# A graph layer with a 17-tap convolution: another start for the first four batches, single conv taps in a ring of nine, and fewer turns of the identity

## The chip, the cores and the metric

The kernel runs on one core of one Trainium2 chip. The metric is the time of one execution on the device in microseconds, the median of several runs. A profiled execution is one more run, taken with the hardware profiler; its trace gives the span from the first to the last instruction. "TensorE" (PE) does matmuls and turns (transposes by a matmul with the identity), "VectorE" (DVE) and "ScalarE" (ACT) elementwise work, "GpSimd" (POOL) small work and DMA issues, "SyncE" (SP) most DMA issues.

## The reference

The layer takes x (32 batches of 512 nodes with 256 channels) and an adjacency matrix of 512x512 for each batch. Everything is fp32. Cut to what is computed:

```python
h  = maximum(layernorm(x), 0)                  # no scale, no shift
xc = transpose(h, (0, 2, 1))                   # channels x nodes
c  = relu(bn1(conv1d(xc, conv1_w, pad=0)))     # 1 tap, 256 -> 256
c  = bn2(conv1d(c, conv2_w, pad=8))            # 17 taps, 256 -> 256
x_conv = transpose(relu(c + xc), (0, 2, 1))
s    = h @ w_se.T + b_se                       # 3 numbers for each node
dist = sq[:, :, None] + sq[:, None, :] - 2 * einsum('bnd,bmd->bnm', s, s)
A    = exp(-dist) * adj                        # sq: sums of s * s
msg  = relu(h @ w_msg.T + b_msg)
x_nmp = einsum('bnm,bmd->bnd', A, msg)
x_in = concatenate([x_conv, x_nmp], axis=-1)
# a GRU cell with input x_in and state h: gates r, z, n
out  = x + (1 - z) * n + z * h
```

## The kernel before

**The parts.** A batch passes through these: `norm` (statistics on VectorE, reciprocal root on GpSimd, the affine on ScalarE, in place), the turn from nodes to channels on the partitions (`norm_t`, L141 on TensorE for the first eight batches, on VectorE for later ones), conv1 (`conv1`, names `ps_g<-hT,w`; its eviction by ScalarE writes `h`), the graph (`graph`: messages `ps_g<-wmsg,hTg`, small factors, four tile-positioned matmuls of 5 rows at L917, `exp` by ScalarE into `at`, four masks multiplied on VectorE, then the gather `ps_g<-at,msg`), and the gates (`gates`, names `ps_acc`).

**The 17-tap convolution** runs over groups of batches. `STARTS` cuts all columns of all batches into seven stages; the first holds four batches (`G = 4`). Within a stage it is a two-level fast convolution: 25 products (`ORDER` x `ORDER`), each with its own combination of inputs (`X2`, made by `operands` on VectorE, names `x`) and its own combination of the weights (`w`). In the first stage the weights are made on the fly by VectorE (`g`, `gg`, from `wraw`), scaled by ScalarE and stored to `WD` in device memory; in later stages they are loaded again. A product has weights 0 and 1, and from the second stage on also their sum, 2, which `third_weight` makes on VectorE once and GpSimd's queue stores. One product, number 6 (`LONE`), needs weight 1 alone. A tile `w` holds all three weights of one product, and three tiles rotate:

```python
    def new_w():
        return cv.tile([P, 3, ND, D], F32, name="w", bufs=3)
```

**The order of the work** is made by a planner that runs when the program is built. Each part is a Python generator, a "stream" (`rows`, `begins`, `graphs`, `conv`, `gates`); the main loop (L1390 and on) picks the stream with the lowest clock among those that are ready by the planner's own estimate of time, `now`, and that stream writes its next instructions into the queues. `fill` adds background work to VectorE's queue while its estimated end is less than 1.5 us ahead: norms, weights (`prepare_some`, at most 3 products ahead), operands (`operand_some`, at most `AHEAD = 3` ahead). Each engine then executes its own queue strictly in that order.

When no stream is ready, `now` goes on by 0.25 us, and until the gates begin TensorE gets turns of the identity into an unused bank (`keep_warm`, L146):

```python
            waits += 1
            if waits > 2 and not HB:
                keep_warm(2)
```

**The start.** Before the loop the planner norms batch 0, then makes the constants of the two batch norms (`bn_affine`, which needs `vecs` loaded and GpSimd's power), then loads batches 1 to 3 (2 and 3 into the space of `y`). The stream `rows` begins with, for each of the first four batches in turn: `begin` (the norm, the two `norm_t`), a wait for ScalarE, then conv1 of that batch. Batch 2 also waits until batch 0's messages are out (`told > 0`). The tile `hT` rotates through two buffers.

**Banks.** TensorE's results for turns, conv1, messages, exps' inputs and gathers share three banks (`gps`), the gates three (`acc`), the convolution two (`cps`, one in the first stage for each product).

Of the kernel before, what the change touches and what calls it, by code (L numbers as in the profile page):

```python
# [8 lines left out]
F32 = mybir.dt.float32  # L9
AF = mybir.ActivationFunctionType  # L10
ALU = mybir.AluOpType
PSUM = bass.MemoryType.PSUM

P = 128
# [35 lines left out]
def kernel(  # L50
# [228 lines left out]
        dve.tensor_scalar(t[:, :n], var, EPS, None, op0=ALU.add)  # L279
        nc.gpsimd.tensor_tensor(dst, t[:, :n], mhalf[:, :n], op=ALU.pow)  # L280

    def bn_affine(name):

        g, bb, m, v = (vec[:, _COL[f"{name}_{k}"] : _COL[f"{name}_{k}"] + ND] for k in "gbmv")
        sc = const.tile([P, ND], F32, name=f"{name}_scale")
        sh = const.tile([P, ND], F32, name=f"{name}_shift")
        rs = front.tile([P, ND], F32, name="bn_rs")
        rsqrt(rs, v)
        dve.tensor_tensor(sc, g, rs, op=ALU.mult)
        t = front.tile([P, ND], F32, name="bn_t")  # L290
        dve.tensor_tensor(t, m, sc, op=ALU.mult)
        dve.tensor_tensor(sh, bb, t, op=ALU.subtract)
        return sc, sh


    h1 = const.tile([P, Q * RV], F32)
# [52 lines left out]
    def norm(b):  # L349

        xs = XS[b]
        st = front.tile([P, NT, 6], F32, name="st")
        mv = front.tile([P, NT, 2], F32, name="mv")
        rstd = front.tile([P, NT], F32, name="rstd")
        shift = front.tile([P, NT], F32, name="shift")
        step = NT // 2 if b == 0 else NT
        for c in range(NT):
            dve.bn_stats(st[:, c, :], xs[:, c, :])
            dve.bn_aggr(mv[:, c, :], st[:, c, :])
            if (c + 1) % step == 0:  # L360
                rsqrt(rstd[:, c + 1 - step : c + 1], mv[:, c + 1 - step : c + 1, 1])
            if c % 2:
                yield dve.free + 2.0 if c == NT - 1 else 0.0
        for c0 in range(0, NT, step):
            k = slice(c0, c0 + step)
            dve.scalar_tensor_tensor(
                shift[:, k], mv[:, k, 0], -1.0, rstd[:, k], op0=ALU.mult, op1=ALU.mult
            )
            yield dve.free + 0.2
            for c in range(c0, c0 + step):  # L370
                act.activation(
                    xs[:, c, :], xs[:, c, :], AF.Identity if b < TURNED else AF.Relu,
                    bias=shift[:, c : c + 1], scale=rstd[:, c : c + 1],
                )
                if c % 2:
                    yield act.free + LAG
# [108 lines left out]
    def operands(g):  # L485

        rv = sizes(g)[3]
        h = h1[:, : Q * rv].rearrange("p (q e) -> p q e", q=Q)
        for x1 in fives(h, 6, rv, lambda: phases("x1", 6, rv, 2), again=True):
            yield None  # L490
            if x1 is not None:
                yield from fives(x1, 2, rv, lambda: phases("x2", 2, rv, 6))

    def ends(x2, rv):

# [25 lines left out]

    WS, W_AT = [], []

    def new_w():
        return cv.tile([P, 3, ND, D], F32, name="w", bufs=3)

    def weights_first():


        outer = [  # L530
            taps_of(
                lambda k, i=i: wraw[:, i, :, :, k, :],
                lambda i=i: prep.tile([P, 2, 3, D], F32, name=f"g{i}", bufs=1),
                True,
            )
            for i in range(ND)
        ]
        for j1 in ORDER:
            g = []
            for o in outer:  # L540
                g.append(next(o))
                yield 0.0
            inner = [
                taps_of(
                    lambda k, i=i: g[i][:, :, k, :],
                    lambda i=i: prep.tile([P, 2, D], F32, name=f"gg{i}", bufs=2),
                    False,
                )
                for i in range(ND)
            ]  # L550
            for j2 in ORDER:
                gg = []
                for i in range(ND):
                    gg.append(next(inner[i]))
                    yield 0.0
                yield dve.free + 0.1
                w = new_w()
                for i in range(ND):
                    act.activation(
                        w[:, :2, i, :], gg[i], AF.Copy, scale=GSCALE[j1] * GSCALE[j2]  # L560
                    )
                nc.scalar.dma_start(WD[len(WS)][:, :2], w[:, :2])
                WS.append(w)
                W_AT.append(act.free + LAG)
                yield 0.0

    def weights_again(m):

        w = new_w()
        k = slice(1, 2) if m % 25 == LONE else slice(0, 2 if m < 50 else 3)  # L570
        nc.sync.dma_start(w[:, k], WD[m % 25][:, k])
        WS.append(w)
        W_AT.append(now + 7.0)

    thirds = set()

    def third_weight(m):
        if m in thirds or m % 25 == LONE:
            return
        thirds.add(m)  # L580
        w = WS[m]
        dve.tensor_tensor(w[:, 2], w[:, 0], w[:, 1], op=ALU.add)
        later(dve.free + 0.4, lambda: nc.gpsimd.dma_start(WD[m % 25][:, 2], w[:, 2]))
        W_AT[m] = dve.free + LAG

    SUMS = []
# [136 lines left out]
            evacuated[b] = PARTS[-1]  # L723
        return True

    AHEAD = 3
    HB_AT, gating = {}, 0
    XC, XC_AT, RES, evacuated = {}, {}, {}, {}
    X2, X_AT, XD = [], [], {}
# [27 lines left out]

    def prepare_some():
        nonlocal prepare_at
        if len(WS) >= 25 or len(WS) >= at_product + 3 or now < prepare_at:  # L760
            return False
        prepare_at = next(prepare)
        return True

    def convolution():
# [3 lines left out]
        def product(ps, *terms, clear=(True, True)):  # L769


            for o in range(ND):
                pairs = [
                    (w[:, k, i, o * P : (o + 1) * P], t[:, at + i * (nu + 1) : at + i * (nu + 1) + nu])
                    for k, t, at in terms
                    for i in range(ND)
                ]
                for n, (lhsT, rhs) in enumerate(pairs):
                    matmul(
                        ps[:, o * nu : (o + 1) * nu], lhsT, rhs,  # L780
                        start=(n == 0 and clear[o]), stop=(n == len(pairs) - 1),
                        skip_group_check=True,
                    )
# [10 lines left out]
        for g in range(NG):  # L794
# [9 lines left out]
            for n in range(25):  # L804
                at_product = m = 25 * g + n
                if n == 6:
                    yield lambda: not EVAC
                while 25 <= len(WS) < min(m + 2, 25 * NG):
                    weights_again(len(WS))
                if m == 24:  # L810
                    yield lambda: len(WS) >= 25
                if late is None and len(WS) >= 25:
# [23 lines left out]
                else:  # L836
                    in_product = True
                    ps = [bank_[:, :nh] for bank_ in pair]
                    if n == LONE:
                        for k in range(2):  # L840
                            product(ps[k], (1, x2[:, 1 - k, :], k), clear=(True, False))
                    else:
                        product(ps[0], (2, x2[:, 1, :], 0), clear=(True, False))
                        act.activation(ps[1], ps[0], AF.Copy)
                        yield act.free + LAG
                        if 25 <= len(WS) == m + 2 < 25 * NG:
                            weights_again(m + 2)
                        for k in range(2):
                            product(ps[k], (k, XD[m][:, k, :], 0), clear=(False, False))
                        del XD[m]  # L850
# [2 lines left out]
                if g > 0:  # L853
                    later(now + 0.3, hand)
                at_product = m + 1
                if 25 <= len(WS) == m + 2 < 25 * NG:
                    weights_again(m + 2)
                yield now
                if g > 0:
                    yield lambda: done is None  # L860
# [109 lines left out]
    def begin(b):  # L970
# [4 lines left out]
        if b >= TURNED:  # L975
# [19 lines left out]
            if b + 2 < B:  # L995
                later(now + 2.0, lambda: load(b + 2))
            return
        if b == 2:
            yield lambda: told > 0
        yield lambda: b not in NORMS  # L1000
        yield NORM_AT[b]
        turning = True
# [292 lines left out]
    def all_graphs():  # L1295
        for b in range(B):
            yield from graph(b)

    def all_begins():
        for b in range(G, B):  # L1300
            yield lambda: b in XS and not rows_wait
            yield from begin(b)
# [1 line left out]
    rows_wait = turning = False  # L1304

    def all_rows():
        nonlocal rows_wait
        for b in range(G):
            yield from begin(b)
            yield act.free + LAG  # L1310
            yield from rows(0, b)
        for g in range(1, NG):
            for b in batches(g):
                yield lambda: (
# [13 lines left out]
    def all_gates():  # L1328
# [5 lines left out]


    streams = {
        "rows": (all_rows(), 1e9, -2.0),
        "begins": (all_begins(), 1.05 * PER, -0.15),
        "graphs": (all_graphs(), 11.5 * PER, -0.5),
# [11 lines left out]
    while 0 in NORMS:  # L1351
        NORM_AT[0] = next(NORMS[0], -1.0)
        if NORM_AT[0] < 0.0:
            del NORMS[0]
    bn1_sc, bn1_sh = bn_affine("bn1")
    bn2_sc, bn2_sh = bn_affine("bn2")
    brz = const.tile([P, 2 * ND], F32)
    dve.tensor_tensor(
        brz, vec[:, _COL["b_ih"] : _COL["b_ih"] + 2 * ND], vec[:, _COL["b_hh"] : _COL["b_hh"] + 2 * ND],
# [5 lines left out]
    dve.tensor_scalar(  # L1365
        bn, vec[:, _COL["b_hh"] + 2 * ND : _COL["b_hh"] + 3 * ND], 0.5, None, op0=ALU.mult
    )
    NORM_AT[0] = act.free + LAG
    load(1)
    spare = cv.tile([P, 9 * NZ], F32, name="y")  # L1370
    for b in (2, 3):
        at = (b - 2) * NT * D
        load(b, spare[:, at : at + NT * D].rearrange("p (c d) -> p c d", d=D))
    nc.sync.dma_start(wmsg[:, :, :D], w_msg)
    nc.sync.dma_start(wmsg[:, :, D:], w_se)
    nc.sync.dma_start(bmsg[:, :D], b_msg.to_broadcast([P, D]))
# [6 lines left out]
    while streams:  # L1383
        names = [k for k in streams if hold[k] is None or hold[k]()]
        able = [k for k in names if ready[k] <= now]
        if not able:
            now += 0.25
            assert now < 1e4
            waits += 1
            if waits > 2 and not HB:  # L1390
                keep_warm(2)
            fill()
            continue
        name = min(able, key=lambda k: clock[k])
# [64 lines left out]
```

## Time and profile before

| | |
|---|---|
| three runs | 2067.52, 2068.64, 2070.0 us; median 2068.64 |
| profiled execution | 2070.59 us |
| its span | 2068.8 us |
| mean granted TensorE clock | 0.994 |
| VectorE, ScalarE busy | 64%, 40% of the span |
| DMA | 378.31 MB, mean 183 GB/s |
| identity turns (L146) | 142, 21.9 us by the profile's modelled ends |
| first 17-tap product starts | 57.5 us |
| waits of TensorE with a named releaser | 15.5 us in all, the two longest 1.8 us each |

How to read it: a group of the timeline starts at its first column and is as long as its second; neighbouring matmuls overlap in the record, since they are pipelined and their ends modelled. The pace of a kind of matmul is therefore read from one group's start to the next group's start. One fp32 matmul appears as two records, a turn as one.

### The profile page before, as it was taken

To read this page: it belongs to the slowest core of one execution; us is meant where nothing else is said; L and a number is where in the kernel's file an instruction comes from. 1 tells how busy PE (TensorE), PEld (TensorE's weight loads), DVE (VectorE), ACT (ScalarE), POOL (GpSimd) and SP (SyncE) were. 2 spreads that over 40 slices of the span, in tenths; PEclk is the share of its full clock that TensorE was granted. 3 is DMA by queue.
4 is the path that set the end of the run, shared out by engine and by line. 5 is a ranking of instruction groups with operands and counts; after the bars stand their busy time and mean duration, and the time that the engine had idled before them with its cause. 6 is when DMAs were issued, how large, how long until landed. Compare 5 with 4: busy or idle time off the path is not lost.

```text
span 2068.8 us, 25327 instructions
## 1 busy us (share of the span) xinstructions
PE 2046.3 (99%) x8724; PEld 1256.4 (61%) x8724; DVE 1319.8 (64%) x2378; ACT 827.0 (40%) x1585; POOL 451.7 (22%) x578
## 2 busy tenths in 40 slices
PE   9999999999999999999999999999999999999998
PEld 5888566666666666665666665566665666644444
DVE  5789677865877667775677663667766576532223
ACT  6544553343543446234353333533344433342221
POOL 2101122321312113221132212322211211132222
PEclk9999999999999999999999999999999999999999
DMA  7455768887889768986799876978776777555554
GB/s 274 162 173 194 250 202 224 190 216 200 193 243 208 195 187 227 211 198 177 189 214 219 188 197 155 227 192 193 171 206 176 184 176 158 148 113 91 68 92 36
DMA packets 539312, 378.31 MB, mean 183 GB/s; under 512 B 452992, under 2 KB 470432, under 8 KB 538048
## 3 DMA queue, kind: packets, MB, share of 16 engines
q1 hardware_dynamic: 381312, 278.74, 47.9%
q0 software_dynamic: 153184, 84.70, 23.9%
q10 hardware_dynamic: 4688, 13.24, 1.7%
q8 instruction: 70, 1.15, 0.2%
q14 instruction: 58, 0.48, 0.1%
HBM read 278.55 MB, written 114.56 MB: 190 GB/s over the span
## 4 chain that ended last, share of the span: by engine, by line
PE 61%; DVE 1%; issue 1%; DMA 0%; POOL 0%; ACT 0%; DVEq 0%; POOLq 0%; ACTq 0%
PE ps_acc L136 36%; PE ps_c L136 13%; PE ps_g L136 10%; PE ps_c L917 1%; PE ps_g L141 0%; DMA cd<-part 0%; DVE y L127 0%; POOL cd L721 0%; DVE part L127 0%; ACT part L127 0%; DVE o_sb L127 0%; DVE right L127 0%; DVE x L127 0%; POOL out_dram L1146 0%; PE ps_g L917 0%
## 5 line engine op out<-in xcount | busy, mean ns | idle before, releaser
L1146 POOL DMA_DIRECT2D out_dram<-o_sb x252 | 276.6, 1733 | 522.1 <-DVE o_sb L127 512.6
L136 PE MATMUL ps_acc<-xconv,wih 128*128 128x512 f32 (+1 forms) x772 | 361.3, 590 | 0.0
L136 PE MATMUL ps_acc<-xnb,wih 128*128 128x512 f32 (+1 forms) x772 | 360.4, 592 | 0.0
L136 PE MATMUL ps_acc<-hTb,whh 128*128 128x512 f32 (+1 forms) x772 | 356.1, 590 | 0.0
L136 PEld LDWEIGHTS ps_c<-xd,w 128*128 128x128 f32 x2304 | 288.6, 191 | 65.2 <-issue 56.2
L136 PEld LDWEIGHTS ps_c<-x,w 128*128 128x128 f32 x2032 | 256.1, 191 | 82.9 <-issue 66.2
L136 PE MATMUL ps_c<-xd,w 128*128 128x135 f32 (+1 forms) x2304 | 291.9, 280 | 0.7 <-ACT ps_c L127 0.4
L136 PE MATMUL ps_c<-x,w 128*128 128x135 f32 (+2 forms) x2032 | 265.3, 279 | 3.1 <-ACT n L127 1.7
L136 PE MATMUL ps_g<-at,msg 128*128 128x512 f32 x512 | 227.0, 593 | 1.3 <-DVE at L127 1.3
L136 PEld LDWEIGHTS ps_acc<-xnb,wih 128*128 128x128 f32 x772 | 141.4, 191 | 140.8 <-issue 137.5
L136 PEld LDWEIGHTS ps_acc<-xconv,wih 128*128 128x128 f32 x772 | 140.7, 190 | 141.6 <-issue 139.7
L136 PEld LDWEIGHTS ps_acc<-hTb,whh 128*128 128x128 f32 x772 | 140.5, 190 | 138.9 <-issue 136.9
L127 DVE TENSOR_TENSOR o_sb<-hTb,r 128x512 f32<-128x512 f32 x63 | 43.4, 689 | 215.6 <-ACT r L127 215.5
L127 DVE TENSOR_TENSOR msg<-ps_g,bmsg 128x256 f32<-128x256 f32 x128 | 54.0, 422 | 190.5 <-PE ps_g L136 190.4
L136 PEld LDWEIGHTS ps_g<-at,msg 128*128 128x128 f32 x512 | 95.0, 190 | 109.4 <-issue 103.8
L127 DVE SCALAR_TENSOR_TENSOR x<-x,x 128x544 f32<-128x544 f32 (+5 forms) x161 | 137.6, 854 | 2.7
L127 DVE TENSOR_TENSOR xd<-x 128x544 f32<-128x544 f32 (+1 forms) x144 | 102.5, 717 | 42.4 <-PE ps_c L136 42.3
L127 DVE TENSOR_TENSOR x<-x 128x272 f32<-128x272 f32 (+5 forms) x280 | 127.1, 498 | 0.3
L136 PE MATMUL ps_g<-wmsg,hTg 128*128 128x259 f32 x496 | 122.3, 381 | 0.0
L136 PE MATMUL ps_g<-hT,w 128*128 128x512 f32 (+8 forms) x296 | 117.6, 545 | 0.0
L127 ACT ACTIVATE ps_c<-ps_c 128x270 f32<-128x270 f32 (+1 forms) x144 | 56.6, 393 | 150.6 <-PE ps_c L136 150.5
L127 ACT ACTIVATE z<-ps_acc,brz 128x512 f32<-128x512 f32 x64 | 43.9, 686 | 179.0 <-PE ps_acc L136 179.0
(124 smaller groups left out, 2354.2 us busy)
## 6 DMA issues: line engine op xcount, KB each, us to landing
w<-wd SPq DMA_DIRECT2D x120, 768.0 KB, 5.6
m_sb<-in_adj_dram SPq DMA_DIRECT2D x384, 64.0 KB, 3.9
hT<-hd SPq DMA_DIRECT2D x33, 512.0 KB, 4.4
hd<-hT POOLq DMA_DIRECT2D x32, 512.0 KB, 6.4
hTb<-hd SPq DMA_DIRECT2D x32, 512.0 KB, 5.3
xnb<-nd SPq DMA_DIRECT2D x64, 256.0 KB, 3.1
out_dram<-o_sb POOLq DMA_DIRECT2D x252, 64.0 KB, 5.0
hTg<-hd SPq DMA_DIRECT2D x31, 512.0 KB, 4.5
```

Source lines behind the costliest of these rows:

```text
L127: getattr(self.engine, name)(*tiles, **more)
L136: nc.tensor.matmul(ps, lhsT, rhs, **more)
L917: nc.tensor.matmul(pss[c], gr.left[k, :], gr.right[k, :], start=True, stop=True, tile_position=(32 * c, 0),)
L1146: nc.gpsimd.dma_start(dst, src, accum_op=ALU.add)
```

## The change

1. In the first four batches, batch 0 aside, the norm's affine runs as `tensor_scalar` on VectorE instead of on ScalarE, without the relu as before (the relu is in the eviction of the turn).
2. `begin` of the first four batches becomes a stream of its own, `firsts`, with the lowest clock; for batches 2 to 5 `begin` waits for batch 0's messages as well as for conv1 of the batch two before. `rows` only waits for its time.
3. `bn_affine` is cut in two: both roots are asked for, then batch 1's load and statistics come, then the rest.
4. A tile `w` holds one weight of one product; nine rotate. A product in the first stage takes two; ScalarE scales and stores each alone. Later each weight is loaded alone, in the order 2, 0, 1, as soon as the tile nine before has been used in the planner's time.
5. Operands may be 4 products ahead (seven tiles `x2` instead of six), weights 5.
6. One identity turn for each fourth quarter microsecond of waiting, instead of two for each quarter after the second.

```diff
-    def bn_affine(name):
+    def bn_affine():
...
+        for name in names:
+            rsqrt(rs[name], parts[name, "v"])
+        yield
...
             for c in range(c0, c0 + step):
+                if 0 < b < G:
+                    dve.tensor_scalar(
+                        xs[:, c, :], xs[:, c, :], rstd[:, c : c + 1], shift[:, c : c + 1],
+                        op0=ALU.mult, op1=ALU.add,
+                    )
+                    if c == NT - 1:
+                        yield dve.free + LAG
+                    continue
                 act.activation(
...
+    RING = 9
+    W_BASE, taken = [], 0
+
     def new_w():
-        return cv.tile([P, 3, ND, D], F32, name="w", bufs=3)
+        nonlocal taken
+        taken += 1
+        return cv.tile([P, ND, D], F32, name="w", bufs=RING)
...
-                w = new_w()
-                for i in range(ND):
-                    act.activation(
-                        w[:, :2, i, :], gg[i], AF.Copy, scale=GSCALE[j1] * GSCALE[j2]
-                    )
-                nc.scalar.dma_start(WD[len(WS)][:, :2], w[:, :2])
+                W_BASE.append(taken)
+                w = [new_w(), new_w()]
+                for k in range(2):
+                    for i in range(ND):
+                        act.activation(
+                            w[k][:, i, :], gg[i][:, k, :], AF.Copy, scale=GSCALE[j1] * GSCALE[j2]
+                        )
+                    nc.scalar.dma_start(WD[len(WS)][:, k], w[k])
...
+    def weights_again():
+        for m in range(25, 25 * NG):
+            W_BASE.append(taken)
+            w = {}
+            for k in (1,) if m % 25 == LONE else (2, 0, 1):
+                yield
+                w[k] = new_w()
+                if k < 2 or m >= 50:
+                    nc.sync.dma_start(w[k], WD[m % 25][:, k])
+            WS.append(w)
+            W_AT.append(now + 7.0)
...
+    def load_weights(done):
+        while len(WS) >= 25 and taken < done + RING and next(again, 0) is None:
+            pass
...
-    AHEAD = 3
+    AHEAD = 4
...
-        if len(WS) >= 25 or len(WS) >= at_product + 3 or now < prepare_at:
+        if len(WS) >= 25 or len(WS) >= at_product + 5 or now < prepare_at:
...
-        if b == 2:
-            yield lambda: told > 0
+        if b < G + 2:
+            yield lambda: b < 2 or told > 0 and rowed > b - 2
...
+    def all_firsts():
+        for b in range(G):
+            yield from begin(b)
+            first_at[b] = act.free + LAG
...
         for b in range(G):
-            yield from begin(b)
-            yield act.free + LAG
+            yield lambda: b in first_at
+            yield first_at[b]
             yield from rows(0, b)
+            rowed = b + 1
...
+        "firsts": (all_firsts(), 1e9, -3.0),
...
-    bn1_sc, bn1_sh = bn_affine("bn1")
-    bn2_sc, bn2_sh = bn_affine("bn2")
+    NORM_AT[0] = act.free + LAG
+    affine = bn_affine()
+    next(affine)
+    load(1)
...
+    next(NORMS[1])
+    NORM_AT[1] = next(NORMS[1])
+    bn1_sc, bn1_sh = next(affine)
+    bn2_sc, bn2_sh = next(affine)
...
-            if waits > 2 and not HB:
-                keep_warm(2)
+            if waits % 4 == 3 and not HB:
+                keep_warm(1)
```

More of the change, by code (lines that the diff above doesn't have):

```diff
@@ L280, in rsqrt @@
         nc.gpsimd.tensor_tensor(dst, t[:, :n], mhalf[:, :n], op=ALU.pow)
-    def bn_affine(name):
[L284 to L293, printed above, removed]
+    def bn_affine():
+        names = ("bn1", "bn2")
+        parts = {
+            (name, k): vec[:, _COL[f"{name}_{k}"] : _COL[f"{name}_{k}"] + ND]
+            for name in names for k in "gbmv"
+        }
+        rs = {name: front.tile([P, ND], F32, name=f"{name}_rs", bufs=1) for name in names}
+        for name in names:
+            rsqrt(rs[name], parts[name, "v"])
+        yield
+        for name in names:
+            sc = const.tile([P, ND], F32, name=f"{name}_scale")
+            sh = const.tile([P, ND], F32, name=f"{name}_shift")
+            dve.tensor_tensor(sc, parts[name, "g"], rs[name], op=ALU.mult)
+            t = front.tile([P, ND], F32, name="bn_t")
+            dve.tensor_tensor(t, parts[name, "m"], sc, op=ALU.mult)
+            dve.tensor_tensor(sh, parts[name, "b"], t, op=ALU.subtract)
+            yield sc, sh
     h1 = const.tile([P, Q * RV], F32)
@@ L491, in operands @@
             if x1 is not None:
-                yield from fives(x1, 2, rv, lambda: phases("x2", 2, rv, 6))
+                yield from fives(x1, 2, rv, lambda: phases("x2", 2, rv, 7))
     def ends(x2, rv):
@@ L565, in weights_first @@
                 yield 0.0
[L567 to L573, printed above, removed]
+    def weights_again():
[9 more added lines that the diff above has]
+            W_AT.append(now + 7.0)
+    again = weights_again()
+    def load_weights(done):
+        while len(WS) >= 25 and taken < done + RING and next(again, 0) is None:
+            pass
     thirds = set()
@@ L581, in third_weight @@
         w = WS[m]
-        dve.tensor_tensor(w[:, 2], w[:, 0], w[:, 1], op=ALU.add)
-        later(dve.free + 0.4, lambda: nc.gpsimd.dma_start(WD[m % 25][:, 2], w[:, 2]))
+        dve.tensor_tensor(w[2], w[0], w[1], op=ALU.add)
+        later(dve.free + 0.4, lambda: nc.gpsimd.dma_start(WD[m % 25][:, 2], w[2]))
         W_AT[m] = dve.free + LAG
@@ L773, in product @@
                 pairs = [
-                    (w[:, k, i, o * P : (o + 1) * P], t[:, at + i * (nu + 1) : at + i * (nu + 1) + nu])
+                    (w[k][:, i, o * P : (o + 1) * P], t[:, at + i * (nu + 1) : at + i * (nu + 1) + nu])
                     for k, t, at in terms
@@ L807, in convolution @@
                     yield lambda: not EVAC
-                while 25 <= len(WS) < min(m + 2, 25 * NG):
-                    weights_again(len(WS))
+                load_weights(W_BASE[m] if m < len(W_BASE) else taken)
                 if m == 24:
@@ L845, in convolution @@
                         yield act.free + LAG
-                        if 25 <= len(WS) == m + 2 < 25 * NG:
-                            weights_again(m + 2)
+                        load_weights(W_BASE[m] + 1)
                         for k in range(2):
@@ L855, in convolution @@
                 at_product = m + 1
-                if 25 <= len(WS) == m + 2 < 25 * NG:
-                    weights_again(m + 2)
                 yield now
@@ L1297, in all_graphs @@
             yield from graph(b)
+    first_at, rowed = {}, 0
+    def all_firsts():
+        for b in range(G):
+            yield from begin(b)
+            first_at[b] = act.free + LAG
     def all_begins():
@@ L1306, in all_rows @@
     def all_rows():
-        nonlocal rows_wait
+        nonlocal rows_wait, rowed
         for b in range(G):
-            yield from begin(b)
-            yield act.free + LAG
+            yield lambda: b in first_at
+            yield first_at[b]
             yield from rows(0, b)
+            rowed = b + 1
         for g in range(1, NG):
@@ L1354 @@
             del NORMS[0]
-    bn1_sc, bn1_sh = bn_affine("bn1")
-    bn2_sc, bn2_sh = bn_affine("bn2")
+    NORM_AT[0] = act.free + LAG
+    affine = bn_affine()
+    next(affine)
+    load(1)
+    spare = cv.tile([P, 9 * NZ], F32, name="y")
+    for b in (2, 3):
+        at = (b - 2) * NT * D
+        load(b, spare[:, at : at + NT * D].rearrange("p (c d) -> p c d", d=D))
+    next(NORMS[1])
+    NORM_AT[1] = next(NORMS[1])
+    bn1_sc, bn1_sh = next(affine)
+    bn2_sc, bn2_sh = next(affine)
     brz = const.tile([P, 2 * ND], F32)
@@ L1367 @@
     )
[L1368 to L1373, printed above, removed]
     nc.sync.dma_start(wmsg[:, :, :D], w_msg)
```

## The prediction

> **What bounds the kernel now.** I read the page first, then TensorE's waits, its timeline, the windows with the clock, and VectorE's and ScalarE's timelines over the first 270 us. The page's first part has this line:
>
> ```profile
> PE 2046.3 (99%) x8724; PEld 1256.4 (61%) x8724; DVE 1319.8 (64%) x2378; ACT 827.0 (40%) x1585; POOL 451.7 (22%) x578
> ```
>
> TensorE is the bound, but "busy" hides three losses: turns of the identity, the half clock, short waits. I priced each group of its timeline at the pace of undisturbed stretches, start to start: 0.109 us for a 128x128 turn, 0.858 for a whole 512-column matmul (two records of 0.429), 0.438 for 259 columns, 0.2225 for 116, 0.2325 for 135 or 136, 1.07 for four tile-positioned 5-row matmuls. Over the program that is 2003.9 us of work plus 142 identity turns (15.5 us). From 280 us on the timeline keeps this pace, with about 9 us lost in the 1790 us that follow, 6.3 of them at two places (461 and 964 us) where the 5-row matmuls stand directly behind conv1 and wait for banks. So the change can win in the first 270 us, where about 44 us are lost, and little elsewhere. TensorE's timeline, columns start, length, group, idle before:
>
> ```profile
> 23.24 3.60 PE L136 MATMUL ps_g<-hT,w 128*128 128x512 f32 x8
> ...
> 31.82 2.39 PE L146 MATMUL ps_acc<-ident 128*128 128x128 f32 x10
> 34.01 5.25 PE L136 MATMUL ps_g<-hT,w 128*128 128x512 f32 x8
> ...
> 41.52 3.69 PE L136 MATMUL ps_g<-hT,w 128*128 128x512 f32 x8
> ...
> 47.03 7.13 PE L136 MATMUL ps_g<-at,msg 128*128 128x512 f32 x16 [0.51 <-DVE at L127]
> ```
>
> See conv1 of batches 1, 2 and 3 at 23.2, 34.0 and 41.5; eight records take 3.4 us, at 34.0 they take 5.1. At 47.0 only 24.1 us of work are done, 22.9 lost. The windows show why 34.0 is slow (us, TensorE busy, clock, DMA share, GB/s):
>
> ```profile
> 28.00:32.00 4.00, 3.67 (x9) 0.81 1.04 343
> 32.00:36.00 4.00, 4.00 (x13) 0.50 0.52 209
> ...
> 260.00:264.00 4.00, 3.75 (x15) 0.50 0.42 126
> ```
>
> Half speed in 30.5 to 37.2 and 259.3 to 266.0 (half-microsecond windows), each 6.7 us long, so 3.4 us lost. VectorE, columns as before:
>
> ```profile
> 39.80 0.69 DVE L127 TENSOR_TENSOR at<-ps_g,at 128x512 f32<-128x512 f32 x1 [8.45 <-PE ps_g L141]
> ...
> 89.91 0.43 DVE L127 TENSOR_TENSOR msg<-ps_g,bmsg 128x256 f32<-128x256 f32 x1 [6.91 <-PE ps_g L136]
> ```
>
> It idles 7 us when TensorE does a gather with messages: nothing may be made further ahead. ScalarE:
>
> ```profile
> 68.96 1.16 ACT L127 ACTIVATE w<-gg 128x512 f32<-128x512 f32 x2
> 70.15 0.33 ACTq L562 DMA_DIRECT2D wd<-w  x1
> 70.53 2.08 ACT L127 ACTIVATE x_sb<-x_sb,shift,rstd 128x256 f32<-128x256 f32 x4 [0.41 <-ACT w L127]
> ```
>
> One tap's weights and their store hold it from 68.96 to 70.53: 1.57 us.
>
> **What the Trainium skill says.** "TensorE: Matmul & The Clock Gate", Part 1, has the clock halve after a window of about 3.4 us with too little activity, and return after a busy one; the two episodes, each of two such windows, agree. Its Part 4 says that transposes do not count as busy in the same way; the trace speaks against it in part, for 103.4 to 108.0 us hold only turns (30 of the identity) and two products' start, at clock 1.00. The windows that did trip hold mostly 5-row matmuls and idle time. "VectorE: DVE Perf Modes", mode 2x_2P, gives an fp32 tensor_scalar twice the rate of a tensor_tensor. No row here shows one of 256 columns.
>
> **The change part by part.** Times are against the profiled execution: span 2068.8, device time 2070.6; the runs' median, 2068.6, lies 2.0 below, and I carry the difference over unchanged.
>
> *Norm on VectorE, own stream, bn work after batch 1's statistics.* Removed from ScalarE: 12 activations of 128x256 at 0.49 (0.98 a pair), 5.9 us between 16.8 and 39.8. Added to VectorE: 12 tensor_scalars, 0.2 (the skill's double rate, an estimate from its section) to 0.35 each (the 256-column message add); I take 0.3, 3.6 us, under its 8.45 us wait. Step by step, durations from the rows of before:
> - To 13.4 us nothing moves: x arrives at 3.60, turns at 7.47, conv1 of batch 0 ends at 13.39.
> - Before, the message adds stood behind batch 2's statistics and began at 16.20; batch 1's norm ran on ScalarE to 19.4 and its turns at 18.66. Now batch 1's statistics come three microseconds earlier and its norm lies between the adds: messages to 17.0, turns to 17.9.
> - The factors need 0.9 on VectorE after the last add: turned by 19.6; conv1 of batch 1 at 19.7, not 23.24 (a wait of 1.11 for hT and 12 identity turns, 1.31, go).
> - It ends at 23.1; turns of batch 2, 0.9; the eight records of 5-row matmuls took 27.64 to 31.8 because ScalarE did a norm pair and hT first; with only relus and hT in front, 24.0 to 26.4. conv1 of batch 2: 26.4 to 29.8, not 34.0 to 39.1.
> - Turns of batch 3 and a mask, 1.3, to 31.1; hT waits for six relus (2.5) and two evictions (1.1): conv1 of batch 3 from 32.2 to 35.6, not 41.5 to 45.0.
> - VectorE then has 7.0 us of g, 2.7 of gg, four mask multiplies of 0.61 and the first operands behind h (36.9): gather at 41.6 with half a product ahead of it, work 25.9. Before reaches that work at 48.8. Gain 7.2.
>
> From this I take 2.7: between conv1 of batch 3 and that half product TensorE has only three mask turns and five identity turns in about 5 us, so a half-clock window is likely (1.7 for one, 3.4 for two). That was also removed, so net +4.5; bounds +1 and +8.
>
> *Fewer identity turns.* 142 become 40 in the instruction order: 102 x 0.109 = 11.1 us, an upper bound. Most stood in front of something not ready; what they covered turns into idle. Nothing is added for them; their possible cost is the clock. The 18 left at the start (30 before) leave TensorE idle from about 5.8 to 7.5, which may keep the first conv1 cold: 0 to 3.4, I take 0.
>
> *Ring of nine, operands 4 ahead, weights 5 ahead.* I counted both orders between gathers with the durations above. Before, four intervals: time 34.9, 32.7, 36.5, 32.9; TensorE's work 33.2, 28.9, 34.2, 29.7; VectorE's 27.9, 24.4, 27.7, 30.9; lost 11.1. After: TensorE 33.2, 34.2, 27.1, 31.5; VectorE 28.5, 27.5, 31.1, 27.4. The third is VectorE's: it stays over TensorE by 4.0, and the interval of before where VectorE led had 2.0 of VectorE idle: 6 lost. The others I price at 1.5, 2.5, 2, near before's 1.7, 3.8, 2.3. Sum 12: cost 1.0. The order agrees that waiting remains: two groups of three identity turns stand in the third interval.
>
> *ScalarE's weights.* Two activations of 512 and one store per tap become four of 256 and two stores. "ScalarE: Activation LUTs", What ACT_TABLE_LOAD costs, prices an immediate one at 186 ns + 0.833 per column, less 93 back to back; for 512 that is 0.61 and 0.52, and the trace shows 0.62 and 0.52. So 256 is 0.40 and 0.31 (estimate): 2 x (0.71 + 0.41) = 2.2 per tap against 1.5, 19 us over 25 taps. It lies in ScalarE's idle time except where weights stand in front of the exps: in graph 1 they do, and the turns of batch 4 behind need a bank that the exps free. About 1.0 us late: cost 1.0, bounds 0 and 5.
>
> *Loads.* 120 loads of 768 KB (5.6 us to landing) become three of 256 KB (4.5 each), 264 more issues on SP, whose queue also holds masks and x blocks. The reload of tap m+2 now goes out at the start of m; taps after 280 us come every 12 us ((2068 - 280)/150). No cost; bounds 0 and 2. POOL's stores of third weights keep their number.
>
> *Into stage 1.* Before loses 2.8 from the fifth to the sixth gather, then 7.3 to 266.0: waits of 1.82 and 1.37 around 5-row matmuls that have little in front, and the second half clock. In the new order those matmuls follow 11.4 us of gate and product work, so these go; I leave 2.5. Ahead of that, twelve mask turns stand in a row, and their four multiplies with y sums between need about 7.2 on VectorE against 3.4 of TensorE's work: 3.7 lost for 2.8. Net +4.8 - 0.9 = +3.9; bounds -2 and +7.
>
> *Later.* The 5-row matmuls stand directly behind conv1 three times (before: twice, 4.9 and 1.4). Two short, one long: 7.7 for 6.3, cost 1.4.
>
> Sum: 4.5 - 1.0 - 1.0 + 3.9 - 1.4 = 5.0 us gained. Own execution 2065.6; median **2063.6**.
>
> **Rivals.**
> - *Look-ahead closes the gaps.* VectorE's 7 us idle stretches fill, the middle loses 6 instead of 12, no half clock (+2.7): 2063.6 - 8.7, about 2055. For it: TensorE's work exceeds VectorE's by 4 in three of four intervals. Against: the third.
> - *ScalarE takes it back.* The weights' 2.2 us stand before all five exps that follow, 1 us each: 5 instead of 1, about 2068, no change. For it: strict order and a store that waits for its own activation (the 0.41). Against: several exps precede the weights.
> - *Half clock, slower.* Too few identity turns to keep 3.4 us windows active: cold first conv1, the first product, the masks before the fourth gather, the twelve turns. Four episodes at 3.4 make 13.6 for the 2.7 priced: 2063.6 + 10.9, about 2074. It decides from the third full episode on (10.2 against 2.7 and the gain of 5.0). For it: both early episodes of before followed such stretches. Against: conv1 of batch 2 comes soon after the 5-row matmuls.
> - That more isn't made ahead is excluded by the order: products start before the first gather.
>
> **How the numbers follow.** 0.2% (4.1 us) is about what runs of this kernel can tell from no change. Forecast 0.40 (own range 2060 to 2067, of it 0.07 within the bound), look-ahead 0.14, ScalarE 0.22 (0.20 within, 0.02 slower), half clock 0.24. Faster 0.33 + 0.14 = 0.47; same 0.27; slower 0.26. The range 2054 to 2075 reaches to the rivals.
>
> **What would show it.** Right: conv1 of batch 3 near 32 to 36, first gather near 42 to 45, at most one half-clock stretch before 60 us, the third interval between gathers longest over its work, no half clock near 260. Wrong: clock 0.50 in more than two stretches before 270; exps waiting behind w; product rows waiting for w loads after 280.

## The result: slower by 0.3%, and the profile after

The changed kernel took 2074.49 us (median of nine runs, 2070.61 to 2079.8); the kernel before took 2067.52 us beside it (nine runs, 2062.53 to 2071.07). The ratio is 1.0029, 95% interval 1.0018 to 1.0041. The forecast, 5.0 us faster, has the wrong sign. The profiled execution after has a span of 2078.0 us and a device time of 2079.8, the slowest of the nine, so its difference to the profile before (9.2 us) is larger than that of the medians (7.0).

The page after, busy time of each engine, then the TensorE clock's windows (columns: us, TensorE busy, weight loads, VectorE, ScalarE, GpSimd, granted clock, DMA share, GB/s):

```profile
PE 2042.2 (98%) x8622; PEld 1248.5 (60%) x8622; DVE 1326.9 (64%) x2390; ACT 830.9 (40%) x1623; POOL 452.0 (22%) x578
```

```profile
40.00:44.00 4.00, 3.35 (x16) 3.38 (x17) 3.93 (x10) 1.45 (x4) 0.00 (x0) 0.57 0.85 320
144.00:148.00 4.00, 1.59 (x2) 0.84 (x3) 3.99 (x9) 2.17 (x6) 0.00 (x0) 0.78 1.02 357
224.00:228.00 4.00, 2.43 (x3) 1.17 (x4) 0.69 (x1) 0.00 (x0) 0.81 (x2) 0.60 0.98 352
228.00:232.00 4.00, 4.00 (x6) 1.47 (x5) 0.00 (x0) 1.27 (x3) 0.49 (x1) 0.55 1.02 382
260.00:264.00 4.00, 4.00 (x17) 2.27 (x16) 3.96 (x9) 4.00 (x7) 0.71 (x2) 1.00 0.42 131
496.00:500.00 4.00, 4.00 (x10) 2.91 (x9) 0.95 (x1) 1.54 (x5) 0.00 (x0) 0.50 0.10 6
```

TensorE is busy for 4.1 us less and yet later at the end. The half speed at 260 is gone; in its place it stands at 10 to 13, 40 to 44, 146 to 150, 225 to 232, 242 to 245, 454 to 457, 494 to 501 and 730 to 733 us. Added over windows of 2 us, (1 - clock) x 2 us makes 10.2 us before and 17.1 after (the last few microseconds, in which TensorE has no work left, aside): about six and ten stretches of 3.4 us at half speed, the length that the Trainium skill ("TensorE: Matmul & The Clock Gate", Part 1) gives for one window.

TensorE's timeline after, the lines that answer to those at 23.2 to 47.0 of before:

```profile
9.46 5.40 PE L136 MATMUL ps_g<-hT,w 128*128 128x512 f32 x8
...
20.26 3.60 PE L136 MATMUL ps_g<-hT,w 128*128 128x512 f32 x8
...
27.40 3.60 PE L136 MATMUL ps_g<-hT,w 128*128 128x512 f32 x8
...
32.96 3.60 PE L136 MATMUL ps_g<-hT,w 128*128 128x512 f32 x8
...
40.65 3.54 PE L136 MATMUL ps_c<-x,w 128*128 128x116 f32 x16 [2.10 <-DVE x L127]
44.02 7.04 PE L136 MATMUL ps_g<-at,msg 128*128 128x512 f32 x16
```

The last conv1 of the start begins at 33.0 instead of 41.5, and the first gather at 44.0 with a whole product ahead of it, instead of 47.0 with none. But the first conv1 is cold (5.40 us for what takes 3.60), and so is the first product.

With the paces of the forecast, start to start, the time that TensorE lost (identity turns counted as lost) can be laid out by stretches of the profile:

| us lost in | before | after |
|---|---|---|
| 0 to 60 | 21.2 | 16.4 |
| 60 to 200 | 10.9 | 10.2 |
| 200 to 280 | 10.1 | 15.3 |
| 280 to the end | 13.7 | 23.8 |
| sum | 56.0 | 65.8 |

These are two single executions, the one after the slowest of its nine. In them the change wins where it works, 5.5 us up to 200 us, and loses 15.3 after that, where apart from how the weights are loaded the diff changes no instruction, only the order. TensorE's waits with a named releaser (us in total, times, longest) show it; before, none was longer than 1.8:

```profile
PE ps_c L136 <- ACT z L127: 6.8, 4, 4.8
PE ps_g L136 <- DVE at L127: 5.5, 2, 3.7
PE ps_g L136 <- DMA hT<-hd: 4.6, 3, 3.1
PE ps_c L136 <- ACT ps_c L127: 2.6, 1, 2.6
PE ps_c L136 <- DVE x L127: 2.1, 1, 2.1
```

Two of them, followed to their source. First, conv1 of the second stage. TensorE, then SyncE's queue:

```profile
218.84 3.61 PE L136 MATMUL ps_g<-hT,w 128*128 128x512 f32 x8
225.57 6.66 PE L136 MATMUL ps_g<-hT,w 128*128 128x512 f32 x8 [3.12 <-DMA hT<-hd]
```

```profile
212.89 0.33 SPq L901 DMA_DIRECT2D whh<-in_w_hh_dram  x1
213.28 0.42 SPq L902 DMA_DIRECT2D wih<-in_w_ih_dram  x1
214.10 0.85 SPq L211 DMA_DIRECT2D hT<-hd  x1
```

The second conv1 waits 3.1 us for the hT that was asked for at 214.10, and that took 11.3 us from issue to landing, where the four such reloads between 195 and 232 us take 4.6 in the median. Directly in front of it in the same queue stand the GRU's weights, 768 and 1536 KB. After the idle time the clock is at half (225 to 232), and the conv1 takes 3.2 us more: the wait is paid twice. In the kernel before, these weights went out at 219.2, 5 us behind that reload:

```profile
214.21 0.32 SPq L211 DMA_DIRECT2D hT<-hd  x1
...
219.20 0.33 SPq L870 DMA_DIRECT2D whh<-in_w_hh_dram  x1
```

Second, the stall at 447 us. TensorE, VectorE, ScalarE:

```profile
447.33 1.26 PE L136 MATMUL ps_g<-hT,w 128*128 128x161 f32 x8
453.38 2.15 PE L136 MATMUL ps_c<-x,w 128*128 128x136 f32 x8 [4.80 <-ACT z L127]
```

```profile
448.62 0.71 DVE L127 STREAM_TRANSPOSE hT<-x_sb 128x512 f32<-128x512 f32 x1 [4.32 <-PE ps_g L136]
449.26 3.58 DVE L127 TENSOR_TENSOR y<-y,z 128x1632 f32<-128x1632 f32 x2
```

```profile
452.94 0.69 ACT L127 ACTIVATE z<-ps_c 128x272 f32<-128x272 f32 x2 [8.30 <-DVE y L127]
```

VectorE's queue holds the turn of a new batch into an hT buffer that the conv1 at 447 still reads; behind that turn stand the additions of y, for these ScalarE's eviction of the last product's bank waits, and for that the next product. All four instructions are in the kernel before as well; there they stand in an order in which the buffer is free. This chain is read from the trace; no run takes it away by itself.

A third kind of loss is one that the prediction named, 5-row matmuls directly behind conv1, here at 491 us:

```profile
491.71 0.69 PE L948 MATMUL ps_c<-right,left 5*128 5x512 f32 x1
...
493.14 1.12 PE L948 MATMUL ps_g<-right,left 5*128 5x512 f32 x2 [0.29 <-ACT h L127]
495.08 3.13 PE L136 MATMUL ps_g<-hT,w 128*128 128x207 f32 x8 [0.82 <-ACT at L127]
```

The waits are short, but the half speed from 494 to 501 comes on top, and the place costs 5.5 us in all.

### The profile page after: what moved, and what is told of

It reads as the page before. It is cut to its first block, busy times and chain, and to the rows that moved or that the text cites. A ratio compares the mean times of both kernels' runs of the same rounds, so it can differ in the third digit from the quotient of the medians.

```text
span 2078.0 us, 25789 instructions
## 1 busy us (share of the span) xinstructions
PE 2042.2 (98%) x8622; PEld 1248.5 (60%) x8622; DVE 1326.9 (64%) x2390; ACT 830.9 (40%) x1623; POOL 452.0 (22%) x578
## 4 chain that ended last, share of the span: by engine, by line
PE 93%; DVE 2%; DMA 2%; ACT 1%; issue 1%; SPq 0%; ACTq 0%; POOL 0%; DVEq 0%; POOLq 0%
PE ps_acc L136 47%; PE ps_c L136 23%; PE ps_g L136 21%; PE ps_g L141 1%; PE ps_c L948 1%; DMA hT<-hd 1%; DMA cd<-part 1%; DVE x L127 0%; DVE g L127 0%; ACT h L127 0%; DMA wd<-w 0%; DVE at L127 0%; PE ps_g L948 0%; DVE z L127 0%; DMA out_dram<-in_x_dram 0%
## 5 line engine op out<-in xcount | busy, mean ns | idle before, releaser
L136 PE MATMUL ps_g<-at,msg 128*128 128x512 f32 x512 | 231.6, 602 | 5.5 <-DVE at L127 5.5
L136 PE MATMUL ps_g<-hT,w 128*128 128x512 f32 (+8 forms) x296 | 123.4, 565 | 6.6 <-DMA hT<-hd 4.6
```

The costliest lines, as they stand in the source:

```text
L136: nc.tensor.matmul(ps, lhsT, rhs, **more)
```

## The experiments

Two explanations stood against each other from the start. *Clock*: the identity turns that the change takes away kept TensorE's clock up. *Waits*: the new order of the work brings waits of its own. The first four kernels take the change apart. The kernel before was run beside each group; its medians were 2067.26, 2067.98 and 2069.71 us in the three groups, so the ratios are what to compare.

**Only the turns put back (e1), only the turns taken away (e2).** The planner's time doesn't depend on the identity turns, so each of the two has TensorE's queue of its counterpart but for them. The traces hold 142 turns before, 40 after, 154 in e1 and 39 in e2, so e1 has 114 more than the changed kernel, not the 102 that its expectation names.

```diff
-            if waits % 4 == 3 and not HB:
-                keep_warm(1)
+            if waits > 2 and not HB:
+                keep_warm(2)
```

> The changed kernel with the identity turns of the kernel before (two for each quarter microsecond of waiting after the second): the same instructions in the same order, and 102 turns of the identity more. Clock theory (too few identity turns let TensorE's clock halve, and that made the change slower): most of the eight half-speed stretches of the changed kernel go, each worth 1.7 us, and the time is 2063 to 2068 us, ratio to before 0.997 to 1.000. Wait theory (the new order's waits, for the reload of hT at 219 and 225 us, for the masks at 142, for z at 447 and for ps_c at 791, made it slower; the turns stand beside waits and cost and bring nothing): 2072 to 2076, ratio 1.002 to 1.004.

> The kernel before with only the fewer identity turns. Clock theory: more half-speed stretches than its three, each 1.7 us or more, less what the 102 turns cost where they stood in front of ready work (2 us): 2070 to 2076, ratio 1.001 to 1.004. Wait theory: no loss, and a gain of up to 3 us from turns that no longer stand in front of ready work: 2064 to 2068, ratio 0.998 to 1.000.

Measured: e1 2077.46 us, ratio 1.0042 (1.0025 to 1.0058); e2 2066.10 us, ratio 0.9992 (0.9984 to 1.0000). The clock theory, that the turns taken away made the change slower, falls: with all turns back the kernel is no faster than without (2074.49), and without them the kernel before is no slower. That half speed costs time doesn't fall with it; it follows other waits too. In e1 the first conv1 is warm again:

```profile
8.95 1.04 PE L146 MATMUL ps_acc<-ident 128*128 128x128 f32 x8
9.82 3.60 PE L136 MATMUL ps_g<-hT,w 128*128 128x512 f32 x8
```

and the half speed of its profile makes 12.0 us instead of 17.1, but its span is 2078.1, that of the changed kernel: the turns themselves take what they save. The stretches from 225 us on are in e1 too (228, 241, 453, 494 to 501, 729), where no kernel here has turns of the identity. Each of them follows a wait or the 5-row matmuls. One at 26 to 30 us is e1's own.

**The start part with the fewer turns (e3), and alone (e4).** The diff is the change's items 1 to 3.

> The start part (norm of batches 1 to 3 on VectorE, own stream, batch norm's constants cut in two) and the fewer identity turns, but the ring of three tiles and the look-ahead of before. Clock theory: the start gains 4 to 5, the clock takes 4 to 8: 2066 to 2072, ratio 0.999 to 1.002. Wait theory, in which the ring's order holds the loss: 2060 to 2064, ratio 0.996 to 0.998.

> The start part alone. The forecast's term for it without its clock price was 7.2 us; it read 2.7 of that as lost if identity turns are few. Both theories: faster than before, 2060 to 2064, ratio 0.996 to 0.998, with conv1 of batch 3 near 33 us and the first gather near 44. A third theory (what the start wins is given back at the next wait, since VectorE and not TensorE sets the pace between the first gathers): 2066 to 2069, ratio 0.999 to 1.000, and the fourth gather no earlier than in the kernel before.

Measured: e3 2075.44, ratio 1.0035 (1.0022 to 1.0047); e4 2079.70, ratio 1.0054 (1.0037 to 1.0070). Every theory missed: without the ring the start part is as slow as the whole change. Yet it does win at the start: up to 60 us e4 loses 15.0 (before 21.2), and e3 14.9 (e2 17.1). From 60 us on e4 loses 47.6 instead of 34.8, e3 42.6 instead of 33.1 (e2).

**The change without its start part (e5), the GRU's weights asked for later (e6), and the 5-row matmuls moved away from conv1 (e7).**

```diff
-        nc.sync.dma_start(whh, w_hh)
-        nc.sync.dma_start(wih, w_ih)
+        later(now + 12.0, lambda: nc.sync.dma_start(whh, w_hh))
+        later(now + 12.0, lambda: nc.sync.dma_start(wih, w_ih))
```

> The changed kernel without its start part: ring of nine single weights, more made ahead, fewer identity turns, on the start of the kernel before. Theory 1 (the start part itself costs, since with it every kernel was 8 to 12 us slower than without): about the time of the fewer turns alone, 2062 to 2068 us, ratio 0.997 to 1.000. Theory 2 (the planner's order from 200 us on is shifted by any edit, and what is lost there is the luck of the new order; the ring shifts it too): anywhere from 2062 to 2078; a ratio over 1.002 shows that the loss isn't the start part's own. Theory 3 (the forecast's middle term, ring costs 1 us against the kernel before, ScalarE's weights 1 more): 2068 to 2070.

> The changed kernel with the two loads of the GRU's weights (whh and wih, 2.25 MB) given to SP's queue 12 us of planner's time later, behind a reload of hT instead of directly in front of it; TensorE's order is unchanged. Theory 1 (conv1 of stage 1 waits at 219 and 225 us because that reload of hT comes to land behind these loads, 11.3 us from issue instead of some 4.6): the 6.2 us of these two waits go, 2067 to 2070, ratio to before 0.9995 to 1.001, and the wait of ps_g on hT falls from 4.6 to under 1.5. Theory 2 (the reloads are late because the ring of two hT buffers lets the next one go out only when conv1 is done): the wait stays above 3, 2073 to 2076.

For e7, besides:

```diff
             conv1(g, b, o)
+            row_at = act.free + 0.3
...
+        if b >= G:
+            yield row_at
         kernel_exp(at)
```

> As e6_gru_later, and from batch 4 on the four 5-row matmuls wait in the planner until ScalarE has evicted the last conv1 (by the planner's own time), so that they aren't put directly behind a conv1 and find their banks taken. Theory 1 (the 5-row matmuls directly behind conv1, at 491 and 727 us, cost 4.4 and 2.5 us with the half clock that follows them): 4 to 7 us faster than e6_gru_later, 2060 to 2065. Theory 2 (any shift of the order loses as much at another place): within 2 us of e6_gru_later or slower.

Measured: e5 2076.10, ratio 1.0038 (1.0023 to 1.0052), so the loss isn't the start part's own. e6 2071.56 (21 runs), ratio 1.0017 (1.0011 to 1.0024): of 7 us it gives back 2.9 in the median, or 2.5 by the ratios, whose intervals overlap; 6.2 were expected. Its profile has the two conv1 without a gap:

```profile
212.10 0.32 SPq L211 DMA_DIRECT2D hT<-hd  x1
212.51 1.26 SPq L599 DMA_DIRECT2D w<-wd  x1
213.94 0.33 SPq L901 DMA_DIRECT2D whh<-in_w_hh_dram  x1
```

```profile
217.67 7.04 PE L136 MATMUL ps_g<-hT,w 128*128 128x512 f32 x16
```

The wait on hT is gone from the list, and from 200 to 280 us it loses 7.3 us instead of 15.3. That the loads stood in front of the reload is thereby shown to be the cause of that wait. The median gains less than the two profiles (9.5 us); the profile of the changed kernel was its slowest run, which may be a part of that. e7 is slower again: 2078.65, ratio 1.0050 (1.0035 to 1.0065). Its 5-row matmuls at the joints cost less (280 to 560 us: 10.7 lost, e6 13.5), but in the new order two reloads of hT come late elsewhere, 4.1 us before the conv1 at 984 and 4.8 before that at 1245, and both conv1 then run at half speed (6.0 and 6.6 us for 3.6):

```profile
PE ps_c L136 <- ACT z L127: 9.1, 4, 4.8
PE ps_g L136 <- DMA hT<-hd: 8.9, 2, 4.8
```

**Order alone: a nudge (e8).** Nothing of the change but the fewer turns, and one starting value of the planner.

```diff
-        "graphs": (all_graphs(), 11.5 * PER, -0.5),
+        "graphs": (all_graphs(), 11.5 * PER, -0.4),
```

> The kernel with the fewer identity turns alone (2066.1 us), and one number of the planner changed that has nothing to do with the change: the stream of the graphs starts with a clock of -0.4 instead of -0.5. The same instructions in another order. Theory of order (the time is set to within several us by how the planner's order happens to fall at the joints of the stages, so that any nudge of the start moves it): differs from 2066.1 by 3 us or more, in either direction. Theory of content (the start part's own work costs the 8 to 12 us): within 2 us of 2066.1.

Measured: 2086.59 us, ratio 1.0088 (1.0071 to 1.0104). That is 20.5 us over e2, which has the same instructions but for eight turns of the identity (47 here, 39 there, 0.9 us). The list of TensorE's waits has much the same kinds as that of the changed kernel, and here a late reload leads it:

```profile
PE ps_g L136 <- DMA hT<-hd: 6.4, 3, 3.4
PE ps_c L917 <- ACT z L127: 2.8, 2, 1.5
PE ps_g L136 <- DVE at L127: 2.8, 2, 2.0
```

**The contents in the old order (e9, e10).** The counterpart: the planner counts the old instructions' time, so that TensorE's queue is that of e2, instruction by instruction. For example:

```diff
+                if 0 < b < G:
+                    act.free = max(act.free, now) + act.fixed + act.each * D
+                    nc.vector.tensor_scalar(
+                        xs[:, c, :], xs[:, c, :], rstd[:, c : c + 1], shift[:, c : c + 1],
+                        op0=ALU.mult, op1=ALU.add,
+                    )
...
-        return cv.tile([P, 3, ND, D], F32, name="w", bufs=3)
+        return [cv.tile([P, ND, D], F32, name="w", bufs=9) for _ in range(3)]
```

> The contents of the change in the old order: the norm's affine of batches 1 to 3 on VectorE, each weight in a tile of its own (ring of nine, four activations of 256 and two stores on ScalarE, single loads), and the fewer identity turns; but the planner counts the time of the instructions that were there before, so that TensorE's queue is that of the fewer turns alone (2066.1 us), instruction by instruction. Nothing more is made ahead. Theory of order: these contents cost next to nothing by themselves, 2063 to 2068, ratio 0.998 to 1.000. Theory of content (ScalarE's longer weights, 264 more DMA issues on SP, and VectorE's affine hold others up): 2071 to 2077, ratio over 1.002.

> As e9_old_order_both without the affine on VectorE: the single weights in the old order, and the fewer identity turns. The forecast's terms of ScalarE's weights (1.0 us lost, bounds 0 and 5) and of the loads (0, bounds 0 and 2) alone, against 2066.1 for the fewer turns: by the forecast 2066 to 2068, by the rival in which ScalarE takes it back (all five exps behind weights late) 2070 to 2072. The difference to e9_old_order_both is the affine on VectorE by itself: 0 to 3 us faster.

Measured: e9 2067.67, ratio 1.0003 (0.9991 to 1.0015); e10 2069.64, ratio 1.0006 (0.9995 to 1.0017). By themselves, single weights and VectorE's affine cost nothing that this measurement can tell from the kernel before; against e2's 0.9992 they may cost 2 to 3 us, and the intervals overlap. e9 and e10 can't be told apart, and e10's time lies between the two expectations. What e9 leaves out of the change, the stream of its own and the greater look-ahead, consists in another order, so it can't be tried with the order held.

**Two more orders (e11 of the change, e12 of the kernel before).** The same starting value at -0.6, in e6 and in e2.

> The changed kernel with the GRU's weights loaded later (e6, 2071.6 us), and the clock of the graphs' stream started at -0.6 instead of -0.5: the same instructions in another order. Theory of order: the change's own time has a spread of several us of the same kind as the kernel before had in e8_nudge; between 2062 and 2082, 2 us or more from e6. Theory that the changed kernel's order is a settled one, and only the order of the kernel before is lucky: within 2 us of e6.

> The kernel of the fewer turns alone (2066.1 us), its graphs' stream started at -0.6 instead of -0.5, the other way than in e8_nudge. Theory of order: slower than 2066.1 by 2 us or more in all likelihood, since the order of the kernel before is the best of many: 2068 to 2082. Theory that e8_nudge was slow because its graphs came later (a trend, not luck): faster than 2066.1, 2055 to 2065.

Measured: e11 2086.15, ratio 1.0082 (1.0066 to 1.0099), 14.6 us over e6 (13.4 by the ratios), more than expected; e12 2070.99, ratio 1.0010 (0.9999 to 1.0021). e11's largest wait is once more a reload, one of 6.2 us at 985:

```profile
PE ps_g L136 <- DMA hT<-hd: 6.2, 1, 6.2
```

So the kernel with the fewer turns takes 2066, 2071 and 2087 us in three orders, the change 2072 and 2086 in two (with the GRU's weights later). e12 also speaks against a trend with the value: a loss of 20 us in one direction isn't a gain in the other. That -0.6 is slower than -0.5 is only just shown, since the intervals of e12 and e2 touch.

No run beats both kernels by more than its interval; the nearest is e2, the fewer identity turns alone in the old order. That an order exists which keeps the 5 us of the start and has none of the late stalls wasn't tried further and stays open.

## Why the prediction was wrong, step by step

- *Start, +4.5: right.* Up to 60 us 4.8 less are lost. conv1 of batch 3 stands at 33.0 (32.2 was forecast), the first gather at 44.0 (41.6) with more done ahead. The 7.2 without the clock's price were 6.2 in e4, the price was 1.7 at the first product and 1.8 at the cold first conv1, which had been priced at 0 (e4 keeps its turns, which count as lost, so these don't simply add). Four tensor_scalars of 256 columns take 1.37 us, 0.34 each, inside the bounds of 0.2 to 0.35; the double rate behind the lower bound isn't seen.
- *Middle, -1.0: near, though of the other sign.* The four intervals between gathers were forecast at 34.7, 36.7, 33.1 and 33.5 us, and took 34.5, 35.3, 32.5 and 33.8. The third lost 5.5 (6.0 forecast), the four together 10.2 (12), where the kernel before lost 11.1: a gain of 0.9.
- *ScalarE's weights, -1.0: right in price, the loss not seen by itself.* 0.42 us for one of 256 columns and 0.72 for two, where 0.40 and 0.71 were worked out; no wait of TensorE behind the exps stands out in the list, and e10 against e2 leaves about 3 us for this and the single loads together (0 to 6 by their intervals).
- *Loads, 0 with bounds 0 and 2: wrong, the first failed step.* I looked at the w loads and at what they are queued behind, not at what else moves in that queue. When all 25 weights are made, the planner also opens the GRU's tiles and asks for 2.25 MB. In the new order these loads went in front of the reload that they follow in the kernel before: 3.1 us of wait and 3.2 of half clock, and 1.7 more at 242 us, where the half speed is gone too in e6. Whether the greater look-ahead brought them forward isn't shown: in e5, which has it, they stand behind that reload, as in the kernel before. The Trainium skill ("DMA: Bandwidth & Descriptors", Queues, rings and completion order) has each DMA engine consume the descriptors of one queue in ring order, though they need not complete in it; the 11.3 us of the reload, and its 4.9 in front of the loads in e6, agree.
- *Into stage 1, +3.9: measured -5.3* (10.1 to 15.3, rounded). In e6, with that one cause taken away, it is +2.8 (10.1 to 7.3): the term's own mechanism was right, the half speed at 260 is gone, and the row of mask turns has waits of 4.2 us in e6, where 3.7 were forecast.
- *Later, -1.4: wrong, the largest failed term, -10.1.* The three places with 5-row matmuls directly behind conv1 were found, and cost 5.5, 3.3 and 1.6 us with the half clock behind the first two (7.7 forecast for the three). Two stalls weren't seen at all: 6.7 us at 447 and 2.8 at 791. I had read the order of the first 270 us closely and carried the old pace over to the rest. The old pace was read too well besides: by the table the kernel before loses 13.7 us from 280 us on, not about 9.
- *The rival that landed nearest, half clock at 2074, was right in part in its mechanism, and in its number by luck.* All four of its episodes came, at about one stretch each instead of two (the last, at 242, isn't in e6), and its sign, half speed in more than two stretches before 270, was seen. But those four make some 7 us of its 13.6; the rest of the loss came from the GRU's loads and from after 280, and e1 shows that putting the turns back doesn't bring the time back. In all three pairs that differ in the turns alone, the kernel with fewer has the lower median.

The base was one profile as well. The forecast removes two losses to half speed from it, 3.4 us each, and not every execution has as much: the kernel before ran at mean clocks from 0.993 to 0.998 (the profile at 0.994), that is with some 14 to 4 us lost to the clock, (1 - clock) of the span. How much of those two losses the median has stays open.

What the forecast lacked was one statement: the order is a result of the planner's own clock, an edit at the start shifts it everywhere after, and the order of the kernel before was the best of the three tried, which differ by up to 20 us. With that, the 5 us won at the start stand against a spread several times as large, and every other order tried has a slower median. Which of the stalls after 280 us make up the median's loss, and why the old order has so few, stays open.

## What to carry to other kernels

Where a program's order comes from a planner that is fed with estimated times, first measure how much the time moves under a change of the planner's starting values that alters no instruction; a part that is worth less than this spread can only be judged with the order held fixed, as e9 does. When the order moves, list everything that waits for the same condition as the part moved: what is released with it may be a large load that goes in front of a small urgent one. A wait of some 3 us on TensorE cost up to twice its length in these traces (3.1 us, then 3.2 more for the conv1 at half speed).

## What was not expected of the hardware

With 103 to 122 turns of the identity fewer, at 0.109 us each, three kernels have medians lower by 1.2 to 4.3 us (each pair's intervals touch or overlap), though the first conv1 went from 3.60 to 5.40 us and the half speed in the profile of the change was 5.1 us more than in that of e1. Keeping the clock up with turns costs about what it saves here, or more. Between runs of the changed kernel the mean granted clock went from 0.991 to 0.995, and the time from 2079.7 to 2072.0 us on average, so two single profiles can differ by some 8 us though the kernel is the same.
